# A selective scan's half groups: the copy of two chunks' sums placed two backward steps later, and two delta loads exchanged

## The chip, the cores and the metric

The kernel runs on one core of a Trainium2 chip. The metric is the device time of one execution in microseconds (us), the median of several runs. The engines are TensorE (PE, with its weight loads shown as PEld), VectorE (DVE), ScalarE (ACT), GpSimd (POOL) and SyncE (SP), whose queue issues the DMA transfers.

## The reference

Four layers run over an image batch `x` of shape (4, 64, 64, 96). The change lies in layer 0, which holds a selective scan over 4096 positions in four directions, with 192 channels and 16 states. Cut to what matters:

```python
def step(h, inp):
    u_t, dt_t, B_t, C_t = inp
    dA = jnp.exp(dt_t[..., None] * A)
    h = dA * h + (dt_t * u_t)[..., None] * B_t[:, None, :]
    y = jnp.sum(h * C_t[:, None, :], axis=-1)
    return (h, y)
# ys over all positions, for x_hw, x_wh and both reversed; the four results are added
```

Layer 1 is a depthwise and a pointwise convolution, layer 2 linear attention and a feed-forward block with float quantization, layer 3 a filter between two Fourier transforms and a second feed-forward block. The kernel works on parts of them beside the scan.

## The kernel before

**Tiling.** A tile of the scan has 128 partitions (8 channels by 16 states) and 1024 positions, a *chunk*; four chunks make the 4096 positions. The three indices (image b, orientation o, group g of 8 channels) give N = 4 x 2 x 24 = 192 values of `n`, which this document calls half groups. In each, VectorE scans the four chunks forward (steps q0 to q3, L1700) and then backward (steps k0 to k3, chunks 3 to 0, L1749), and adds the backward result to the forward one (L1759). A backward scan's last value goes to the next through `edge` (L1755).

**What a half group needs.** `load_delta` and `load_du` (both through L1413) fetch a chunk each, in two DMAs of 256 KB. `decay` (L1458, ScalarE) makes exp(delta times A) in PSUM; there are two such buffers, used in turn, and six decays a half group, since those of chunks 2 and 3 serve both directions. `times_b` (L1441) and `times_c` (L1445), on GpSimd, multiply by B and C in place. `reduce` (L1472, PE) adds up the 16 states by matmuls into `py`, one bank of PSUM of which there is a single buffer; `result` (L1480, ScalarE) copies it out, and `store_result` (L1489) stores it with four DMAs. A half group has two such rounds: half 0 for chunks 0 and 1, half 1 for chunks 2 and 3.

**Where the sums stand.** The sums of half 1 of `n` are reduced at k3 of the same half group and copied at q0 of the next. Those of half 0 are reduced in the next half group: chunk 1 at q1, chunk 0 at q3; they are copied at k0, ahead of that step's scan, and stored at k1.

**A second form from half group 55 on.** Once the lane of the other images' preparation is done (`"pre" in done`), the backward scan of chunk 0 writes into the delta tile `dls[n, 0]` instead of being added; `times_c_apart` (L1450) multiplies it, and the reduction of chunk 0 reads it as a second term. The place of that delta tile is then in use until that reduction.

**Places.** Delta tiles have five places, dl0 to dl4. `place_of` gives chunk q the place q in even half groups and 4, 3, 2, 1 in odd ones; the tiles `S` of the scans follow the same rule. So chunks 1 to 3 of the next half group take places of the current one as these come free, and chunk 0 takes the fifth. The du tiles have eight places.

**Order.** The loop writes the order of all engines out by hand (a manual schedule). Every queue runs its instructions in that order, SP's too. After the scan of each step, `pieces(step)` puts in work of the other layers ("pieces" of lanes) as far as the step's credit for each engine goes; its DMAs go through the same SP queue. The loads of the loop on SP, in order, are: q0 du(n+1, 2); q1 du(n+1, 3); q2 delta(n+1, 2) and the store of half 1; q3 delta(n+1, 1); k0 delta(n+1, 0); k1 the store of half 0 and du(n+2, 0); k2 delta(n+1, 3); k3 du(n+2, 1). The decays stand at q0, q1, q2 (chunks 1, 2, 3), k1 (chunk 1 again), k2 (chunk 0 again) and k3 (chunk 0 of n+1).

Of the kernel before, what the change touches and what calls it, by code (L numbers as in the profile page):

```python
# [10 lines left out]
F32 = mybir.dt.float32  # L11
# [35 lines left out]
CH = 1024  # L47
# [26 lines left out]
def layers(ctx: ExitStack, tc: tile.TileContext, a: dict, out):  # L74
# [1294 lines left out]
    def last_place(name, k):  # L1369

        if (name, k) not in last_tiles:
            tags = {
                "w_in": [f"B{4 * (N % 2) + q}" for q in range(4)],
                "sz_in": [f"dl{place_of(*x)}" for x in ((N - 1, 3), (N - 1, 2), (N - 1, 1), (N, 0))],
                "xr": [f"rep0{q}" for q in range(4)],
                "y_in": [f"B{4 - 4 * (N % 2) + q}" for q in range(4)],
            }
            t = big.tile([128, CH], F32, tag=tags[name][k // 2], name=name)
            for j in range(2):
                last_tiles[name, k // 2 * 2 + j] = t[:C, j * BLK : (j + 1) * BLK]  # L1380
        return last_tiles[name, k]
# [16 lines left out]
    N = len(phases)  # L1398
    dls, Bs, Ss, reps, pys, yss = {}, {}, {}, {}, {}, {}

    def place_of(n, q):


        return (4, 3, 2, 1)[q] if n % 2 else q

    def channel_halves(t):

        return [t[k * 64 : k * 64 + 64, :] for k in range(2)]

    def load_channels(t, src, g, q):  # L1410
        for k, part in enumerate(channel_halves(t)):
            rows = src[g * 8 + k * 4 : g * 8 + k * 4 + 4, chunk(q)]
            nc.sync.dma_start(part, rows.unsqueeze(0).broadcast_to([NS, 4, CH]))  # L1413

    def load_delta(n, q):
        if n < N:
            b, g, o = phases[n]
            t = dls[n, q] = big.tile([128, CH], F32, tag=f"dl{place_of(n, q)}", name="dl")
            load_channels(t, delta_s[o][b], g, q)

    def load_du(n, q):
        if n < N:
            b, g, o = phases[n]

            at = 4 * (n % 2) + (3 - q if n % 4 > 1 else q)
            t = Bs[n, q] = big.tile([128, CH], F32, tag=f"B{at}", name="B")
            load_channels(t, du_s[o][b], g, q)
# [24 lines left out]
    def decay(n, q, first):  # L1452

        if n < N:
            tag = "pa" + "XY"[(n + (not first)) % 2]
            pa = ps.tile([128, CH], F32, tag=tag, name="pa")
            g = phases[n][1]
            nc.scalar.activation(pa, dls[n, q], AF.Exp, scale=nega[:, g : g + 1])  # L1458
            return pa

    def reduce(n, half, chunks=(0, 1)):

        if n < 0:
            return
        if (n, half) not in pys:
            pys[n, half] = ps.tile([128, BLK], F32, tag="py", name="py")
        py = pys[n, half]
        for j in (2 * c + k for c in chunks for k in range(2)):
            q, k = 2 * half + j // 2, j % 2
            terms = [Ss[n, q]] + ([dls[n, 0]] if q == 0 and n in apart else [])  # L1470
            for i, x in enumerate(terms):
                nc.tensor.matmul(  # L1472
                    py[32 * j : 32 * j + 32, :], lhsT=red, rhs=x[:, k * BLK : (k + 1) * BLK],
                    start=(i == 0), stop=(i == len(terms) - 1),
                )

    def result(n, half):
        if n >= 0:
            ys = yss[n, half] = big.tile([128, BLK], F32, tag="ys", name="ys", bufs=2)
            nc.scalar.copy(ys, pys.pop((n, half)))  # L1480

    def store_result(n, half):
        if n < 0:
            return
        b, g, o = phases[n]
        ys = yss.pop((n, half))
        for j in range(4):
            i = 4 * half + j
            nc.sync.dma_start(  # L1489
                y_s[o][b][g * 8 : g * 8 + 8, i * BLK : (i + 1) * BLK], ys[32 * j : 32 * j + 8, :]  # L1490
            )
# [114 lines left out]
    big = core.enter_context(tc.tile_pool(name="scan", bufs=1))  # L1606
# [60 lines left out]
    with tc.manual_schedule():  # L1667
        ordered[0] = True
        pas = [decay(0, 0, True), None, None, None]
        for n in range(N + 1):  # L1670
            h = n // NG
            end = n == N

            for q in range(NCH):

                if q < 2:
                    load_du(n + 1, q + 2)
                else:
                    load_delta(n + 1, 4 - q)
                if n % NG == 0 and 0 < n < N and q > 0:  # L1680
                    load_rep(h, 1, 4 - q)
                if q < 3:
                    pas[q + 1] = decay(n, q + 1, q == 1)
                if q == 0:
                    times_b(n, 3)
                elif q == 1:
                    times_c(n - 1, 0)
                    reduce(n - 1, 0, (1,))
                elif q == 2:
                    times_c_apart(n - 1)  # L1690
                    store_result(n - 1, 1)
                else:
                    times_b(n + 1, 0)
                    reduce(n - 1, 0, (0,))
                if end:
                    if q == 0:
                        result(n - 1, 1)
                    continue
                s = Ss[n, q] = big.tile([128, CH], F32, tag=f"S{place_of(n, q)}", name="S")
                nc.vector.tensor_tensor_scan(  # L1700
                    s, pas[q], Bs[n, q], Ss[n, q - 1][:, CH - 1 : CH] if q else 0.0,
                    ALU.mult, ALU.add,
                )
                pieces(q)
                if q == 0:
                    result(n - 1, 1)
            if end:
                result(n - 1, 0)
                store_result(n - 1, 0)
                break  # L1710
            if n % NG == 0 and n > 0:
                load_rep(h, 1, 0)
            if n % NG == 1 and n > 1:
                b, o = halves[h - 1]
                if o == 1:
                    done["columns", b] = True
                if h % 2 == 0 and b < NB - 1:
                    done["scans", b] = True
            if n == N - NG // 2 + 1:
                done["half", NB - 1] = True  # L1720

            for k, q in enumerate(reversed(range(NCH))):
                if k < 2:
                    times_b(n + 1, k + 1)
                if k > 0:
                    times_c(n, q + 1)
                if k == 0:
                    result(n - 1, 0)
                    load_delta(n + 1, 0)
                elif k == 1:  # L1730
                    store_result(n - 1, 0)
                    load_du(n + 2, 0)
                elif k == 2:
                    load_delta(n + 1, 3)
                else:
                    load_du(n + 2, 1)
                if n % NG == NG - 2:
                    load_rep(h + 1, 0, k)
                if k == 1:
                    pas[1] = decay(n, 1, False)  # L1740
                elif k == 2:
                    pas[0] = decay(n, 0, True)
                elif k == 3:
                    first = decay(n + 1, 0, True)


                alone = k == 3 and "pre" in done
                to = dls[n, 0] if alone else pas[q]
                nc.vector.tensor_tensor_scan(  # L1749
                    to[:, ::-1], pas[q][:, ::-1], Bs[n, q][:, ::-1],  # L1750
                    edge if k else 0.0, ALU.mult, ALU.add,
                )
                if k < 3:
                    edge = big.tile([128, 1], F32, tag="edge", name="edge", bufs=2)
                    nc.vector.tensor_copy(edge, to[:, 0:1])  # L1755
                if alone:
                    apart.add(n)
                else:
                    nc.vector.tensor_tensor(Ss[n, q], Ss[n, q], to, ALU.add)  # L1759
                if k == 3:  # L1760
                    reduce(n, 1)
                pieces(4 + k)
                if n == N - 1:
                    for i in (2 * k, 2 * k + 1):
                        last_loads(last_place, i)
            pas[0] = first
            if n % NG == NG - 4 and h + 1 < len(halves):
                b, o = halves[h + 1]
                assert done.get(("turns", b)) if o else done.get(("back", b)) == NBLK, (n, done)
# [118 lines left out]
```

## Time and profile before

| what | value |
|---|---|
| median of 3 runs | 5872.94 us (5869.17 to 5878.88) |
| the profiled execution | 5867.99 us, its span 5866.2 us |
| scan loop within the span | about 359 to 5421 us |
| forward scan, 128x1024 | 2.28 us (first chunk) and 2.35 us |
| backward scan, 128x1024 | 2.30 us (first) and 2.35 us |
| add of both directions | 1.21 us |
| decay on ScalarE | 1.12 us |
| product on GpSimd | 2.36 us |
| copy of half a half group's sums | 0.58 us |
| share of the 16 DMA engines over the span | 72.5% |
| mean granted TensorE clock | 0.778 |

Times are read from one profiled execution. Idle time of an engine is put down to what ended it; a wait for several things is put down to the one that came last. Lines such as L1480 are those of the kernel.

### The profile page before, as it was taken

How to read it: one execution, taken by the hardware profiler on the slowest of the kernel's cores; microseconds unless marked ns; L12 is line 12 of the kernel's file. 1: busy time of each engine (PE TensorE's matmuls, PEld its weight loads, DVE VectorE, ACT ScalarE, POOL GpSimd, SP SyncE). 2: the span in 40 equal slices, each digit the busy share in tenths (PEclk: the TensorE clock that was granted, in tenths of full speed). 3: DMA queues.
4: the chain of work that ended last, by engine and by line, in shares of the span. 5: the costliest groups of instructions: out<-in, count | busy, mean ns of one | idle time of the engine just before them, and what ended most of it. 6: DMA issues, size and time to landing. Idle time of an engine off the chain costs nothing. (4 is left out here: it accounts for less than half of the span.)

```text
span 5866.2 us, 64908 instructions
## 1 busy us (share of the span) xinstructions
PE 4369.5 (74%) x20038; PEld 1680.1 (29%) x20038; DVE 4801.4 (82%) x3479; ACT 3018.7 (51%) x4141; POOL 4413.7 (75%) x2118
## 2 busy tenths in 40 slices
PE   8978898799884776664566776667678667667888
PEld 3322222222220221142331221245222114333345
DVE  2049889889889888999889999999988999979364
ACT  4557666676555346645444546434444554424233
POOL 0258888789879778988778989888897898867200
PEclk9979889899886776666777876668678766767888
DMA  3258868887679878788988867679987578886003
GB/s 100 77 155 237 233 200 229 224 233 214 199 218 246 226 201 224 208 247 239 251 234 227 227 178 214 191 211 251 233 230 205 164 210 233 242 230 194 23 37 105
DMA packets 469417, 1173.13 MB, mean 200 GB/s; under 512 B 90496, under 2 KB 155628, under 8 KB 468972
## 3 DMA queue, kind: packets, MB, share of 16 engines
q1 hardware_dynamic: 469068, 1168.97, 72.5%
q8 instruction: 159, 2.61, 0.2%
q14 instruction: 190, 1.56, 0.1%
HBM read 1011.86 MB, written 156.76 MB: 199 GB/s over the span
## 5 line engine op out<-in xcount | busy, mean ns | idle before, releaser
L1445 POOL TENSOR_TENSOR S<-S,rep 128x1024 f32<-128x1024 f32 x768 | 1807.9, 2356 | 580.6 <-DVE S L1759 496.6
L1441 POOL TENSOR_TENSOR B<-B,rep 128x1024 f32<-128x1024 f32 x768 | 1798.3, 2357 | 107.8 <-DMA B<-du_s 67.8
L1458 ACT ACTIVATE pa<-dl,nega 128x1024 f32<-128x1024 f32 x1152 | 1283.9, 1116 | 1148.3 <-DVE S L1759 717.7
L1700 DVE TENSOR_TENSOR_SCAN S<-pa,S,B 128x1024 f32<-128x1024 f32 x576 | 1352.2, 2348 | 286.8 <-ACT pa L1458 117.2
L1472 PE MATMUL py<-S,red 128*32 128x512 f32 x3072 | 927.4, 845 | 667.2 <-POOL S L1445 456.8
L1749 DVE TENSOR_TENSOR_SCAN pa<-pa,edge,B 128x1024 f32<-128x1024 f32 x439 | 1032.1, 2351 | 67.9 <-ACT pa L1458 67.3
L361 PE MATMUL p_conv<-xp,conv_w 96*96 96x504 f32 (+3 forms) x2304 | 1054.4, 611 | 6.9 <-ACT u L374 4.9
L1759 DVE TENSOR_TENSOR S<-S,pa 128x1024 f32<-128x1024 f32 x631 | 764.7, 1212 | 1.9
L1700 DVE TENSOR_TENSOR_SCAN S<-pa,B 128x1024 f32<-128x1024 f32 x192 | 436.7, 2275 | 225.8 <-ACT pa L1458 179.9
L361 PEld LDWEIGHTS p_conv<-xp,conv_w 96*96 96x96 f32 x2304 | 382.2, 170 | 674.2 <-issue 636.5
L1480 ACT COPY ys<-py 128x512 f32<-128x512 f32 x384 | 222.8, 580 | 546.4 <-PE py L1472 487.3
L1749 DVE TENSOR_TENSOR_SCAN pa<-pa,B 128x1024 f32<-128x1024 f32 x192 | 440.9, 2296 | 5.4
L1472 PEld LDWEIGHTS py<-S,red 128*32 128x32 f32 x3072 | 111.8, 125 | 1148.0 <-POOL S L1445 647.4
L154 ACT COPY side<-side 96x256 f32<-96x256 f32 (+1 forms) x448 | 279.5, 628 | 127.8 <-DMA deltaT_s<-side 46.5
L1749 DVE TENSOR_TENSOR_SCAN dl<-pa,edge,B 128x1024 f32<-128x1024 f32 x137 | 320.7, 2341 | 14.6 <-ACT pa L1458 14.6
L1450 POOL TENSOR_TENSOR dl<-dl,rep 128x1024 f32<-128x1024 f32 x137 | 323.2, 2359 | 0.1
L1055 POOL CAST h<-y 128x1536 fp8e5<-128x1536 f16 x64 | 95.6, 1494 | 296.9 <-ACT y L766 273.6
L1472 PE MATMUL py<-dl,red 128*32 128x512 f32 x548 | 243.5, 752 | 30.3 <-POOL dl L1450 30.1
L877 PE MATMUL p_mean<-t,centre 96*96 96x512 f32 x256 | 172.6, 787 | 98.1 <-ACT sq L869 48.9
L527 PE MATMUL p_y<-side,ident 96*96 96x512 f32 x336 | 208.8, 771 | 24.3 <-DVE q L920 10.0
L833 PE MATMUL p_l<-x,taps 96*96 96x504 f32 (+3 forms) x432 | 202.3, 619 | 14.9 <-DMA x<-x 12.5
L458 POOL TENSOR_TENSOR r<-r,side 96x512 f32<-96x512 f32 x16 | 20.2, 1263 | 249.0 <-ACT side L443 248.8
(214 smaller groups left out, 5580.4 us busy)
## 6 DMA issues: line engine op xcount, KB each, us to landing
B<-du_s SPq DMA_DIRECT2D x768, 256.0 KB
dl<-delta_s SPq DMA_DIRECT2D x768, 256.0 KB
B<-duT_s SPq DMA_DIRECT2D x768, 256.0 KB
dl<-deltaT_s SPq DMA_DIRECT2D x768, 256.0 KB
z_s<-z SPq DMA_DIRECT2D x48, 512.0 KB
zl<-z_s SPq DMA_DIRECT2D x64, 384.0 KB
side<-y_s SPq DMA_DIRECT2D x120, 192.0 KB
rep<-bc_s SPq DMA_DIRECT2D x64, 256.0 KB
```

The costliest lines, as they stand in the source:

```text
L154: nc.scalar.copy(o.rearrange("p (w h) -> p w h", h=HW), t[:n, :].rearrange("p (h w) -> p w h", w=HW)[:, q * w : (q + 1) * w, :],)
L361: nc.tensor.matmul(pr[:, ra:rb, ca_:cb_], lhsT=conv_w[:, kc, ky * 3 + kx, oc * C : (oc + 1) * C], rhs=xp[:, kc, at + ra : at + rb, ca_ + d ...
L527: nc.tensor.matmul(p, lhsT=ident[:C, :C], rhs=x, start=(j == 0), stop=(j == 2))
L1441: nc.gpsimd.tensor_tensor(Bs[n, q], Bs[n, q], reps[n // NG, 0, q], ALU.mult)
L1445: nc.gpsimd.tensor_tensor(Ss[n, q], Ss[n, q], reps[n // NG, 1, q], ALU.mult)
L1450: nc.gpsimd.tensor_tensor(dls[n, 0], dls[n, 0], reps[n // NG, 1, 0], ALU.mult)
L1458: nc.scalar.activation(pa, dls[n, q], AF.Exp, scale=nega[:, g : g + 1])
L1472: nc.tensor.matmul(py[32 * j : 32 * j + 32, :], lhsT=red, rhs=x[:, k * BLK : (k + 1) * BLK], start=(i == 0), stop=(i == len(terms) - 1),)
L1480: nc.scalar.copy(ys, pys.pop((n, half)))
L1700: nc.vector.tensor_tensor_scan(s, pas[q], Bs[n, q], Ss[n, q - 1][:, CH - 1 : CH] if q else 0.0, ALU.mult, ALU.add,)
L1749: nc.vector.tensor_tensor_scan(to[:, ::-1], pas[q][:, ::-1], Bs[n, q][:, ::-1], edge if k else 0.0, ALU.mult, ALU.add,)
L1759: nc.vector.tensor_tensor(Ss[n, q], Ss[n, q], to, ALU.add)
```

## The change

The sums of chunk 0 are reduced at k0 instead of q3; the sums of half 0 are copied at k2 behind that step's decay instead of at k0, and stored at k3 instead of k1. Behind the last half group the same three steps stand one after another. Delta of chunk 0 of the next half group is loaded at q2 instead of k0, and delta of chunk 2 at k1 instead of q2; chunks 1 and 3 keep their steps. The delta places follow a list in place of `place_of`: the next half group's chunks 0 to 3 take the places of the current chunks 2 and 3, the spare place and the place of chunk 1, and the current chunk 0's becomes spare. The tiles `S` keep `place_of`. The place of one group of late loads for the end of the kernel (`sz_in`) is named by the same list.

```diff
-                "sz_in": [f"dl{place_of(*x)}" for x in ((N - 1, 3), (N - 1, 2), (N - 1, 1), (N, 0))],
+                "sz_in": [
+                    f"dl{delta_places[n][q]}" for n, q in ((N - 1, 3), (N - 1, 2), (N - 1, 1), (N, 2))
+                ],
...
+    delta_places, spare = [(0, 1, 2, 3)], 4
+    while len(delta_places) <= N:
+        p = delta_places[-1]
+        delta_places.append((p[2], p[3], spare, p[1]))
+        spare = p[0]
...
-            t = dls[n, q] = big.tile([128, CH], F32, tag=f"dl{place_of(n, q)}", name="dl")
+            t = dls[n, q] = big.tile([128, CH], F32, tag=f"dl{delta_places[n][q]}", name="dl")
...
                 if q < 2:
                     load_du(n + 1, q + 2)
                 else:
-                    load_delta(n + 1, 4 - q)
+                    load_delta(n + 1, q - 2)
...
                 else:
                     times_b(n + 1, 0)
-                    reduce(n - 1, 0, (0,))
...
             if end:
+                reduce(n - 1, 0, (0,))
                 result(n - 1, 0)
                 store_result(n - 1, 0)
...
                 if k == 0:
-                    result(n - 1, 0)
-                    load_delta(n + 1, 0)
+                    reduce(n - 1, 0, (0,))
                 elif k == 1:
-                    store_result(n - 1, 0)
                     load_du(n + 2, 0)
+                    load_delta(n + 1, 2)
                 elif k == 2:
                     load_delta(n + 1, 3)
                 else:
+                    store_result(n - 1, 0)
                     load_du(n + 2, 1)
...
                 elif k == 2:
                     pas[0] = decay(n, 0, True)
+                    result(n - 1, 0)
```

## The prediction

> **What bounds the kernel now.** I read the page first (busy times and the costliest groups), then the stretches before and after the reductions get their second matmul pair, then who waits for the copy and for the queue, and last the timeline around single stalls.
>
> ```profile
> PE 4369.5 (74%) x20038; PEld 1680.1 (29%) x20038; DVE 4801.4 (82%) x3479; ACT 3018.7 (51%) x4141; POOL 4413.7 (75%) x2118
> ...
> L1700 DVE TENSOR_TENSOR_SCAN S<-pa,S,B 128x1024 f32<-128x1024 f32 x576 | 1352.2, 2348 | 286.8 <-ACT pa L1458 117.2
> ...
> L1749 DVE TENSOR_TENSOR_SCAN pa<-pa,edge,B 128x1024 f32<-128x1024 f32 x439 | 1032.1, 2351 | 67.9 <-ACT pa L1458 67.3
> ...
> L1480 ACT COPY ys<-py 128x512 f32<-128x512 f32 x384 | 222.8, 580 | 546.4 <-PE py L1472 487.3
> ```
>
> VectorE carries the scans, and nothing overlaps a scan of the same engine. The windows of the two stretches of the scan loop show its load there:
>
> ```profile
> 359.00:1861.00 1502.00, 1249.38 (x3098) 385.35 (x3099) 1314.61 (x840) 963.51 (x1312) 1284.57 (x646) 0.85 0.79 221
> 1861.00:5421.00 3560.00, 2435.56 (x12872) 970.85 (x12870) 3239.71 (x2230) 1717.29 (x2322) 2984.45 (x1361) 0.72 0.81 220
> ```
>
> The columns are length, then PE, PEld, DVE, ACT, POOL busy, clock, DMA share, GB/s. VectorE is busy 1314.6 of 1502 us (87.5%) and 3239.7 of 3560 us (91%), so about 187 + 320 = 507 us of its idle time lie in the loop. Only idle time of VectorE can be won. Two kinds of it touch the change. The first, from the timeline of half group 12:
>
> ```profile
> 688.49 1.05 PE L1472 MATMUL py<-S,red 128*32 128x512 f32 x4
> ...
> 689.59 0.58 ACT L1480 COPY ys<-py 128x512 f32<-128x512 f32 x1 [7.89 <-PE py L1472]
> 690.19 1.28 ACT L399 ACT_TABLE_LOAD   x1
> ...
> 693.51 1.28 ACT L107 ACT_TABLE_LOAD   x1
> 694.80 1.12 ACT L1458 ACTIVATE pa<-dl,nega 128x1024 f32<-128x1024 f32 x1
> ...
> 695.96 2.36 DVE L1749 TENSOR_TENSOR_SCAN pa<-pa,edge,B 128x1024 f32<-128x1024 f32 x1 [2.87 <-ACT pa L1458]
> ```
>
> The copy of step k0 stands at ScalarE's head for 7.89 us until PE reaches the reduction of chunk 0; four other instructions and the decay of k1 are queued behind it, and the backward scan of k2 starts 2.87 us late. The second, from half group 60:
>
> ```profile
> 1958.56 1.16 SPq L1413 DMA_DIRECT2D dl<-deltaT_s  x2
> ...
> 1965.57 2.15 ACT L1458 ACTIVATE pa<-dl,nega 128x1024 f32<-128x1024 f32 x2 [9.89 <-DMA dl<-deltaT_s]
> ...
> 1966.78 2.29 DVE L1700 TENSOR_TENSOR_SCAN S<-pa,B 128x1024 f32<-128x1024 f32 x1 [6.40 <-issue]
> ```
>
> Here delta of chunk 0 is issued late, lands at about 1965.5, and the next half group's first scan loses 6.40 us. The DMA queue's own waits name two that the change moves (total us, times, longest):
>
> ```profile
> SPq L1413 <- PE py L1472: 182.5, 61, 10.2
> ...
> SPq L1489 <- ACT ys L1480: 117.3, 44, 9.2
> ```
>
> **What the Trainium skill says.** "PSUM — Partial Sum Buffer", Engine vs sequencer instructions: the queues of ScalarE, VectorE and GpSimd are strict FIFO. The 7.89 us above agrees: work that needs nothing from PE waits behind the copy. "DMA: Bandwidth & Descriptors", Anatomy of one DMA: a semaphore wait happens on the issuing sequencer, before dispatch. The 182.5 us agree: one load that waits for PE holds every load behind it. "ScalarE: Activation LUTs", What ACT_TABLE_LOAD costs: about 1283 ns a load, and a drain besides; the trace has 1.28 us, twice in the chain above. "Perfetto Trace Analysis", Optimization Strategy: find the gaps on the contended engine and the instruction that ends them, which is how the sums below are made.
>
> **The change part by part.** No instruction is added or removed; steps are q0 to q3 (forward) and k0 to k3 (backward).
>
> 1. *Copy of chunks 0 and 1 from k0 to k2, behind the last decay.* Taking all scans of the loop in order, and calling a scan stalled when its idle time exceeds 0.32 us and its decay ended within 0.25 us of its start: in the first 55 half groups the scan of k2 is stalled 25 times, 52.9 us in all (the later ones: 7 times, 9.4 us). Following each back along ScalarE's order, the copy's wait stands in the chain in 21 of the 25, with 40.4 us. With the copy at k2 the table load, two activations and a table load (1.28+1.06+1.04+1.28 us) can start up to 8 us earlier, as in half group 12, so the stall itself goes. What is late next in that stretch is PE: forward scans there already wait 14.3 us for reductions, and PE is busy 83%. I take three quarters of 40.4: **30 us** (10 to 45).
>
> 2. *The copy in its new place.* It is 0.58 us of ScalarE behind the decay of chunk 0 and ahead of the pieces of k2. That decay can start when the scan of k2 starts (k1's add is over), 7.1 us after k0's first scan. PE ends the reduction of chunk 0 at a median of 1.3 us after that scan in the first stretch (90%: 4.3, worst 7.7), 0.2 in the second (90%: 3.7). Moved behind pieces(3), whose PE credit is 2.0, I add 2 to 4 us: at worst 11.7, mostly under 8. So the copy seldom waits, and the next half group's first decay, which needs k2's add at 10.7, hides it. The reduction of chunks 2 and 3 at k3 needs the same single bank of PSUM, free at about 7.1+1.1+0.6 = 8.8 us, but also the product of chunk 2 on GpSimd, ready at 7.1+2.36 = 9.5: nothing. Without that cover it would cost PE 1 to 2 us a half group, which VectorE would see only in part.
>
> 3. *Reduction of chunk 0 from q3 to k0.* Its matmuls had 38 us of PE waiting ahead of them in all (4.6 and 33.8 us by stretch); pieces(3) no longer stand behind that. Nothing else: 0 us (-5 to +5).
>
> 4. *Delta of chunk 0 from k0 to q2.* It goes to the place of the current chunk 2, free after the decay of q1, some 7 us ahead of k0, so it has 18 us to land where it had 11 less the wait for PE. Late arrivals of it now: 16 stalls of the next first scan, 42.5 us, all in the second stretch. They go.
>
> 5. *Delta of chunk 2 from q2 to k1.* It takes the spare place, which the reduction of chunk 0 frees in the half groups with the separate product, and it is queued behind du of n+2. Queued behind its wait for PE: delta 3, the store, du and the pieces' transfers. The du load it now follows was issued 5.8 us (median), 9.0 (75%) and 12.7 (90%) after k0's scan in the second stretch; ahead of it a delta load and a store (1.2 and 1.3 us) disappear. A delta load takes 5.3 us to land (median), and the decay has to start by 16.9 us, so it must be issued by about 11. That leaves nearly a tenth of 136 half groups, 13, late by 2 us: 26 us back on f2. Also, the stretches with late loads have the DMA engines at 86 to 93% and delta 3 lands there with 0 to 3 us to spare, so part of item 4 only moves on to q2's scans. Net of 4 and 5: 42.5 - 26 = 16, less a little for delta 3: **13 us** (-60 to +45; the lower end is the rival below).
>
> 6. *Store from k1 to k3.* Four issues, 1.3 us; the wait of 117.3 us for the copy leaves du of k1. The du load of k3 now stands behind it, at 8.8 us or later, where it was issued at a median of 10 to 11: within 2 us, hidden by GpSimd's waits for VectorE (496.6 us over the run). 0 us (-10 to 0).
>
> Sum: 30 + 13 = 43 us. The profiled execution took 5867.99 us (span 5866.2, 1.8 around it): 5825. The median shown, 5872.94, is 5 us above that execution, so **5830 us**.
>
> **The rivals.**
> - *A, as above, in whole or in part*, 15 to 75 us won: 5830, own range 5798 to 5858. For it: the stalls are on VectorE itself and their causes are in the moved instructions.
> - *B, all of it and more.* The 42.5 and 40.4 us go whole, and with them 14.3 us of stalls by delta 3 at q3, since the queue isn't held at k0: 97 us, 5776. Against it: a late queue in those stretches has other causes (ScalarE's decays alone hold it 268.0 us).
> - *C, refilled.* What is won at k2 is lost at the next forward scans to PE, and what is won at the first scan to the DMA engines: within 10 us of 5873. For it: PE at 83% in the first stretch, DMA at 90% where loads are late.
> - *D, slower: delta of chunk 2 becomes the late load.* Place: the decay of q1 and the scan of q2. It decides when the load at k1 is issued later than 11 us after k0's scan in over a quarter of the second stretch: 35 half groups by 3 us are 105 us, less the 72 of items 1 and 4: 33 us slower, 5906. For it: one more load is queued ahead of it than of chunk 0 before, its place hangs on PE, and delta 3, issued right behind it, is already late 13 times. Against it: the decay of q1 comes 5 us later than the one it replaces as the tightest.
>
> **How the numbers follow.** A 0.55, B 0.10, C 0.14, D 0.21. A change of 0.2%, 12 us, is about what can be told from none. A and B win more than that nearly always: faster 0.66. C is mostly inside it: same 0.13. Slower 0.21. The range for 8 in 10 takes A, C, half of B and most of D: 5785 to 5898.
>
> **What would show it.** Item 1: idle time of L1749 for decays falls from 67.3 us to under 25, and the copies' wait for PE from 487.3 to under 150. Item 4: no first forward scan waits for delta. Item 5: decays of q1 that wait for delta, none today; over 30 of them, or over 60 us, prove D. If the waits fall but the idle time of L1700 grows by as much, C is right.

## The result and the profile after

The changed kernel took 5849.50 us (5844.06 to 5857.01, 5 runs), against 5872.96 us before (5 runs): ratio 0.9965, 95% interval 0.9952 to 0.9978. It is 23 us faster, where the forecast was 43. Two later measurements of the same kernel, each beside the kernel before on the same chip, gave 0.9943 (0.992 to 0.9965, 28 us) and 0.9949 (0.9929 to 0.9968, 33 us). So by the medians the gain is 23 to 33 us, and 10 to 20 us of the forecast are missing. (The ratios are not the quotients of these medians; by them the three gains are 21, 33 and 30 us, and their intervals together reach from 13 to 47 us.)

These lines of the page of the changed kernel answer to those shown of before (L1708 is now the forward scan, L1759 the backward scan, L1467 the decay, L1481 the reduction, L1489 the copy, L1422 the loads, L1498 the store, L1769 the add):

```profile
PE 4352.3 (74%) x20038; PEld 1673.5 (29%) x20038; DVE 4799.4 (82%) x3479; ACT 3016.6 (52%) x4141; POOL 4412.4 (75%) x2118
...
L1708 DVE TENSOR_TENSOR_SCAN S<-pa,S,B 128x1024 f32<-128x1024 f32 x576 | 1352.2, 2348 | 316.2 <-ACT pa L1467 146.0
...
L1759 DVE TENSOR_TENSOR_SCAN pa<-pa,edge,B 128x1024 f32<-128x1024 f32 x439 | 1031.9, 2351 | 40.4 <-ACT pa L1467 40.4
...
L1489 ACT COPY ys<-py 128x512 f32<-128x512 f32 x384 | 221.8, 578 | 9.8 <-PE py L1481 7.5
```

The copies no longer wait for PE: 487.3 us became 7.5. Of the 67.3 us that the backward scans lost to decays, 27 are gone. But the forward scans of q1 to q3 now lose 146.0 us to decays instead of 117.2: more than what the backward scans won. The gain lies elsewhere, in the first forward scans, whose line is this before and then after:

```profile
L1700 DVE TENSOR_TENSOR_SCAN S<-pa,B 128x1024 f32<-128x1024 f32 x192 | 436.7, 2275 | 225.8 <-ACT pa L1458 179.9
```

```profile
L1708 DVE TENSOR_TENSOR_SCAN S<-pa,B 128x1024 f32<-128x1024 f32 x192 | 436.4, 2273 | 188.9 <-DMA rep<-bc_s 169.8
```

Their idle time fell by 36.9 us. (One wait of about 170 us at the start of the loop is in both.) The windows of the two stretches say where the time changed; the first stretch ends at the first scan of half group 56, and the columns are as before:

```profile
358.30:1857.80 1499.50, 1253.00 (x3092) 387.92 (x3096) 1313.68 (x840) 964.04 (x1312) 1282.25 (x646) 0.85 0.80 221
1857.80:5402.60 3544.80, 2411.72 (x12879) 961.67 (x12873) 3238.12 (x2230) 1714.31 (x2322) 2985.02 (x1361) 0.73 0.82 221
```

The first stretch, where the copy's 30 us were to be won, is only 2 us shorter; the second, where only delta was to win, is 15 us shorter. (By the means of all profiles in the table below, three of the changed kernel and two of before, it is 10 and 19 us.) The single cases shown of before are both cured. Half group 12, in the timeline:

```profile
687.94 2.30 DVE L1759 TENSOR_TENSOR_SCAN pa<-pa,B 128x1024 f32<-128x1024 f32 x1
...
691.10 1.05 PE L1481 MATMUL py<-S,red 128*32 128x512 f32 x4
691.48 2.35 DVE L1759 TENSOR_TENSOR_SCAN pa<-pa,edge,B 128x1024 f32<-128x1024 f32 x1
...
695.07 2.35 DVE L1759 TENSOR_TENSOR_SCAN pa<-pa,edge,B 128x1024 f32<-128x1024 f32 x1
695.19 1.12 ACT L1467 ACTIVATE pa<-dl,nega 128x1024 f32<-128x1024 f32 x1 [2.12 <-DVE S L1769]
696.24 0.58 ACT L1489 COPY ys<-py 128x512 f32<-128x512 f32 x1
```

The reduction ends at 692.15, 4.2 us after the scan of k0 begins; nobody waits for it, and the copy follows the decay of k2 without a gap. The scan of k2 (695.07) stands directly behind k1's add. And half group 60, whose first scan lost 6.40 us to delta:

```profile
1948.86 1.53 SPq L1422 DMA_DIRECT2D dl<-deltaT_s  x2
...
1955.52 1.12 ACT L1467 ACTIVATE pa<-dl,nega 128x1024 f32<-128x1024 f32 x1 [1.96 <-DVE S L1769]
1957.66 2.27 DVE L1708 TENSOR_TENSOR_SCAN S<-pa,B 128x1024 f32<-128x1024 f32 x1
```

The decay now waits for VectorE's own add, and the first scan starts without idle time.

For what follows, each scan ahead of which VectorE stood idle for over 0.32 us is counted by its step and by the cause, as in the prediction; the wait of 170 us at the start of the loop is left out. "Late" means that the scan's decay ended within 0.25 us of the scan's start; "delta" means that this decay had itself waited for a load of delta. "PE idle" is time in which PE did nothing ahead of an instruction of one set, summed over 54 half groups of the first stretch: the reduction of chunk 0 and the pieces of q3, which are the work that the change puts in the other order. All values are us of one profiled execution each.

| kernel | first stretch | k2 late | q0 + q1 late | PE idle | second stretch | q0 delta | q2, q3 delta |
|---|---|---|---|---|---|---|---|
| before | 1501.9 | 52.9 | 12.0 | 6.9 | 3559.9 | 42.5 | 14.4 |
| before, second profile | 1505.4 | 56.5 | 10.9 | 8.1 | 3560.0 | 43.7 | 11.4 |
| changed | 1499.5 | 24.7 | 36.7 | 17.9 | 3544.8 | 0 | 43.6 |
| changed, second | 1493.2 | 24.2 | 28.7 | 17.8 | 3539.8 | 0 | 41.0 |
| changed, third | 1489.5 | 20.7 | 26.1 | 19.0 | 3539.0 | 0 | 38.9 |
| sums_only | 1495.7 | 30.0 | 24.8 | 20.7 | 3559.7 | 54.1 | 11.2 |
| copy_only | 1479.6 | 23.1 | 14.7 | 8.3 | 3574.5 | 54.7 | 13.4 |
| deltas_only | 1512.1 | 52.8 | 17.2 | 7.2 | 3547.5 | 0 | 45.7 |
| sum_at_q3 | 1483.4 | 26.5 | 17.5 | 5.2 | 3548.7 | 0 | 44.4 |
| sum_at_q3, second | 1478.3 | 23.8 | 17.4 | 8.2 | 3549.8 | 0 | 39.5 |
| sum_at_q3_d2_k0 | 1477.6 | 26.3 | 12.4 | 7.9 | 3541.4 | 0 | 25.1 |
| first_q3 | 1492.4 | 29.4 | 19.4 | 6.5 | 3529.8 | 0 | 32.4 |
| sum_at_k1 | 1493.2 | 25.4 | 36.2 | - | 3539.6 | 0 | 39.6 |
| reduction_alone | 1535.4 | 108.6 | 6.2 | 16.5 | 3573.0 | 33.0 | 14.3 |

A row stands for one execution, which need not be a typical one: that of copy_only took 5867.38 us, the longest of its 19 (median 5848.43), that of sum_at_q3 5842.53, the longest of its 6 (5832.15), and that of sum_at_k1 5841.17, the shortest of its 22 (5855.66).

Two things stand in the rows of the changed kernel. The stall of k2 fell by 28 to 32 us, as forecast, and late decays of q0 and q1, which grew by 14 to 25 us, took much of it back.

### The profile page after: what moved, and what is told of

Its sections match the earlier page's. It is cut to its first block, busy times and chain, and to the rows that moved or that the text cites. A ratio compares the mean times of both kernels' runs of the same rounds, so it can differ in the third digit from the quotient of the medians.

```text
span 5852.6 us, 65288 instructions
## 1 busy us (share of the span) xinstructions
PE 4352.3 (74%) x20038; PEld 1673.5 (29%) x20038; DVE 4799.4 (82%) x3479; ACT 3016.6 (52%) x4141; POOL 4412.4 (75%) x2118
## 5 line engine op out<-in xcount | busy, mean ns | idle before, releaser
L1467 ACT ACTIVATE pa<-dl,nega 128x1024 f32<-128x1024 f32 x1152 | 1286.0, 1117 | 1448.0 <-DVE S L1769 1089.6
L1708 DVE TENSOR_TENSOR_SCAN S<-pa,S,B 128x1024 f32<-128x1024 f32 x576 | 1352.2, 2348 | 316.2 <-ACT pa L1467 146.0
L1481 PE MATMUL py<-S,red 128*32 128x512 f32 x3072 | 894.9, 837 | 673.6 <-POOL S L1454 460.9
L1759 DVE TENSOR_TENSOR_SCAN pa<-pa,edge,B 128x1024 f32<-128x1024 f32 x439 | 1031.9, 2351 | 40.4 <-ACT pa L1467 40.4
L1769 DVE TENSOR_TENSOR S<-S,pa 128x1024 f32<-128x1024 f32 x631 | 764.6, 1212 | 1.9
L1708 DVE TENSOR_TENSOR_SCAN S<-pa,B 128x1024 f32<-128x1024 f32 x192 | 436.4, 2273 | 188.9 <-DMA rep<-bc_s 169.8
L1759 DVE TENSOR_TENSOR_SCAN pa<-pa,B 128x1024 f32<-128x1024 f32 x192 | 440.8, 2296 | 5.4
L1481 PEld LDWEIGHTS py<-S,red 128*32 128x32 f32 x3072 | 108.5, 124 | 1142.0 <-POOL S L1454 629.7
L1759 DVE TENSOR_TENSOR_SCAN dl<-pa,edge,B 128x1024 f32<-128x1024 f32 x137 | 320.7, 2341 | 18.3 <-ACT pa L1467 11.2
L527 PE MATMUL p_y<-side,ident 96*96 96x512 f32 x336 | 217.6, 798 | 41.5 <-DVE side L561 12.4
L1481 PE MATMUL py<-dl,red 128*32 128x512 f32 x548 | 222.7, 736 | 21.2 <-POOL dl L1459 21.2
L1489 ACT COPY ys<-py 128x512 f32<-128x512 f32 x384 | 221.8, 578 | 9.8 <-PE py L1481 7.5
```

Source lines behind the costliest of these rows:

```text
L1481: nc.tensor.matmul(py[32 * j : 32 * j + 32, :], lhsT=red, rhs=x[:, k * BLK : (k + 1) * BLK], start=(i == 0), stop=(i == len(terms) - 1),)
L1708: nc.vector.tensor_tensor_scan(s, pas[q], Bs[n, q], Ss[n, q - 1][:, CH - 1 : CH] if q else 0.0, ALU.mult, ALU.add,)
L1759: nc.vector.tensor_tensor_scan(to[:, ::-1], pas[q][:, ::-1], Bs[n, q][:, ::-1], edge if k else 0.0, ALU.mult, ALU.add,)
```

## The experiments

Three theories were on record. P: PE paces the first stretch whatever the order, so what is won at k2 is lost at the next forward scans (rival C of the prediction). R: it is the reduction, moved from q3 to k0, that makes PE late for those scans. S: the small gain of the first stretch is scatter of one execution. Every experiment below was timed beside the kernel before on the same chip.

**The change taken apart.** The changed kernel again, and its parts alone:

```diff
# sums_only: reduction k0, copy k2, store k3 of the change; delta loads and places as before
# copy_only: as sums_only, and the reduction stays at q3
                     times_b(n + 1, 0)
+                    reduce(n - 1, 0, (0,))
...
                 if k == 0:
-                    reduce(n - 1, 0, (0,))
                     load_delta(n + 1, 0)
# deltas_only: delta loads and places of the change; reduction q3, copy k0, store k1 as before
```

> The changed kernel once more, for the spread of one profiled execution. The first stretch of the scan loop (to the first scan of half group 56) lasted 1501.9 us before and 1499.5 us after, the second 3559.9 and 3544.8 us. Theory P (in the first stretch PE, with the stretches in which its clock is lowered, sets the pace, so that the stall taken from the scan of k2 comes back at the next forward scans): first stretch again 1496 to 1502 us. Rival S (the first stretch is won in most executions and was not in the one profiled): 1475 to 1490 us. Both: ratio to before 0.995 to 0.998.

> Reduction of chunk 0, copy and store moved as in the change; delta loads and places as before. P: nothing won in the first stretch (1496 to 1502 us); in the second, the load of delta 0 at k0 now waits for a reduction that comes 1 to 3 us later, so first forward scans lose more to delta than the 42.5 us of before: whole time 0 to 15 us over before. Rival S: 10 to 25 us won in the first stretch, whole time 5855 to 5870.

> Only the copy (k0 to k2) and the store (k1 to k3) moved; the reduction of chunk 0 stays at q3, delta loads as before. P: first stretch 1495 to 1502 us, whole time within 8 us of before. Rival R (the refill comes from the reduction, which in its new place stands in PE's queue ahead of the next group of convolution matmuls): the first stretch keeps the gain, 1472 to 1485 us, whole time 5845 to 5858.

> Only delta loads and places changed; reduction at q3, copy at k0 and store at k1 as before. All theories: first stretch as before (1498 to 1505 us), copies wait for PE about 487 us as before. P: the second stretch alone carries the gain of the change, 12 to 25 us, whole time 5848 to 5861. S and R: it carries less than that, 0 to 12 us.

Measured, against 5868.31 us for the kernel before: after_again 5840.74 (0.9943, 0.992 to 0.9965); sums_only 5865.22 (0.9993, 0.9983 to 1.0003); copy_only 5848.43 (0.9964, 0.9952 to 0.9976); deltas_only 5860.36 (0.9985, 0.9975 to 0.9995).

The copy alone (with the store) wins 20 us. With the reduction moved as well, only 3 us are left; the two intervals don't overlap, and the two kernels differ in that one step. A later reduction could also have held up the load of delta at k0, as the expectation of sums_only had it, but the first scans' waits for delta are the same in both, 54.1 and 54.7 us. P fails for copy_only: its k2 stalls fell to 23.1 us, q0 and q1 stayed at 14.7, and the first stretch was 22 us shorter than before. (In that one long execution the second stretch was 15 us longer than before, so the 20 us rest on the median of 19 executions.) The deltas alone win 8 us, which fits all three theories.

S was right in part. after_again's first stretch, 1493.2 us, lies between what P and S expected, and its ratio is below the expected 0.995. But the first stretch of sums_only, 1495.7 us, is at the edge of P's bounds and far from the 10 to 25 us that S expected to be won there.

**The change without the moved reduction.**

```diff
# sum_at_q3, against the changed kernel
                     times_b(n + 1, 0)
+                    reduce(n - 1, 0, (0,))
...
             if end:
-                reduce(n - 1, 0, (0,))
                 result(n - 1, 0)
...
                 if k == 0:
-                    reduce(n - 1, 0, (0,))
+                    pass
# sum_at_q3_d2_k0: as above, and
                 if k == 0:
+                    load_delta(n + 1, 2)
                 elif k == 1:
                     load_du(n + 2, 0)
-                    load_delta(n + 1, 2)
```

> The whole change but for one step: the reduction of chunk 0 stays at q3; copy at k2, store at k3 and both delta loads as in the change. R (the moved reduction stands in the middle of PE's convolution work and gives back what the copy wins): 10 us or more below the changed kernel, 5820 to 5838 us against 5868 before (ratio 0.992 to 0.995), the first stretch below 1490 us. P (PE with its half-clock episodes paces the first stretch whatever the order): as the changed kernel, 5840 to 5850, first stretch 1493 to 1500. S (what was seen is scatter from run to run): within 5 us of the changed kernel, either side.

> As sum_at_q3, and delta of chunk 2 is loaded at k0, a step sooner than in the change (its place is free there once the reduction stands at q3). If the load is late because it is issued behind du at k1, the second stretch's waits of the scans of q2 and q3 for delta, 43.6 us in the changed kernel, fall below 15 us and the kernel is 20 to 30 us below sum_at_q3. If the DMA engines are what is late (they are at 86 to 93% there), the waits stay above 30 us or come back at the first scan, and the time is within 8 us of sum_at_q3.

Measured, against 5868.98: sum_at_q3 5832.15 (0.9929, 0.9909 to 0.9948), sum_at_q3_d2_k0 5831.45 (0.9931, 0.9912 to 0.9949). As R expected, 37 us below before, and the first stretch at 1483.4 and 1477.6. Loading delta of chunk 2 a step sooner cured the waits of q2 (20.6 us to none) but not those of q3 (23.8 and 25.1), so the waits fell from 44.4 to 25.1 us and not to under 15, and the time did not move. The window of the first stretch of sum_at_q3:

```profile
357.00:1840.40 1483.40, 1238.41 (x3092) 383.82 (x3096) 1313.51 (x840) 963.63 (x1312) 1282.50 (x646) 0.85 0.80 224
```

What the reduction does at q3 and at k0 is to be seen in half group 41. First the timeline of the changed kernel, then that of sum_at_q3, at the same step:

```profile
1465.64 2.71 PE L361 MATMUL p_conv<-xp,conv_w 96*96 96x512 f32 x6
...
1468.98 0.91 ACT L305 ACTIVATE xb<-xb,gn 96x640 f32<-96x640 f32 x1
...
1469.94 0.78 PE L313 MATMUL p_xp<-xb,w_in 96*96 96x320 f32 x2 [1.58 <-ACT xb L305]
1470.65 1.20 PE L1481 MATMUL py<-S,red 128*32 128x512 f32 x4
...
1471.78 2.02 PE L361 MATMUL p_conv<-xp,conv_w 96*96 96x512 f32 x2
```

```profile
1453.64 2.71 PE L361 MATMUL p_conv<-xp,conv_w 96*96 96x512 f32 x6
...
1456.28 1.05 PE L1481 MATMUL py<-S,red 128*32 128x512 f32 x4
...
1456.98 0.91 ACT L305 ACTIVATE xb<-xb,gn 96x640 f32<-96x640 f32 x1
...
1457.94 0.78 PE L313 MATMUL p_xp<-xb,w_in 96*96 96x320 f32 x2 [0.60 <-ACT xb L305]
1458.56 2.73 PE L361 MATMUL p_conv<-xp,conv_w 96*96 96x512 f32 x6
```

PE runs its work in the written order. In the first stretch this order is the same in both kernels, but for the place of the moved reduction. At q3 PE has to wait for ScalarE's `xb` in any case. With the reduction at q3 its 1.05 us lie in that wait, and 0.60 us of idle time are left. With the reduction at k0 PE idles for 1.58 us and does the reduction afterwards, ahead of the next convolution. The same 0.60 against 1.58 us stands in half groups 20, 22, 37, 39 and 41 of both kernels; two others (17, 49) have 1.41 against none, where PE waits for ScalarE's `r`. The table's column "PE idle" sums it up: 5.2 to 8.3 us in all kernels with the reduction at q3, 16.5 to 20.7 with it at k0. (The last line of the changed kernel's timeline is slow for another reason: the granted clock was 0.50 there, and 1.00 in the last line of sum_at_q3's.)

PE's lateness shows at the half groups right behind, in four of five cases. By the mean, 21, 38, 40 and 42 take 1.4 to 2.7 us longer in the kernels with the copy at k2 and the reduction at k0 (the changed kernel three times, sums_only) than in those with it at q3 (copy_only, sum_at_q3 twice, sum_at_q3_d2_k0, first_q3). In these four half groups late decays of q0 and q1 cost 7.0 to 13.7 us with the reduction at k0, and 0 to 1.5 us with it at q3. Over the whole first stretch they cost 29.1 us by the mean against 16.3. Following ScalarE's order back from each of these late decays, its last wait was one for PE in 21 to 29 us of them with the reduction at k0, and in 10 to 12 us with it at q3. So the 13 us between the two sets come by way of PE. The granted clock doesn't tell them apart: it is 0.85 to 0.86 over the first stretch in all nine profiles.

**What PE's time is worth.** In both kernels 8 of the 18 matmuls of each convolution of images 1 to 3 are left out, so that their sums are no longer those of the reference:

```diff
                         at = r0 + dy - lo
+                        if b > 0 and k % 2 and k < 17:
+                            continue
                         nc.tensor.matmul(
```

> Before, with 8 of the 18 matmuls of each convolution of images 1 to 3 left out (the credit they are counted at is kept, so the order stays): PE has some 375 us less to do in the first stretch. P: PE paces a good part of the stretch, so it becomes at least 60 us shorter (5868 to 5810 or less). R: PE only delays what stands behind it at single places: 15 to 50 us shorter. The wait of the copies for PE at k0 must fall under both, since PE reaches the reduction sooner: to under 250 us.

> The changed kernel with the same 8 of 18 matmuls left out. P and R: with PE's load gone the moved reduction costs nothing, and the copy's stall at k2 is smaller in both kernels; what is left of the difference to before_light is the delta part, 9 us, plus what of the copy's wait was not PE's load: 5 to 20 us below before_light. If instead the reduction at k0 costs time for a reason other than PE's queue, after_light is not below before_light.

Measured: before_light 5777.49 (0.9839, 0.9824 to 0.9855), after_light 5764.81 (0.9825, 0.9807 to 0.9843). The first stretches, before_light and after_light:

```profile
359.20:1775.10 1415.90, 1028.43 (x2330) 278.38 (x2331) 1312.29 (x839) 965.81 (x1312) 1283.05 (x646) 0.75 0.84 235
```

```profile
356.80:1773.60 1416.80, 1020.58 (x2329) 276.88 (x2329) 1312.04 (x840) 963.96 (x1312) 1282.81 (x646) 0.75 0.83 234
```

With 221 us less PE work (1249 to 1028; the expected 375 was too much) the stretch is 86 us shorter, where R expected 15 to 50 and P at least 60, and the two kernels are equal in it. With PE at 73% the copy at k0 costs no more than that at k2 (stalls of k2: 14.0 us in before_light, 18.0 in after_light), although copies still wait 52.6 us for PE in that stretch (136.3 before), and the moved reduction costs nothing either (late decays of q0 and q1: 7.8 and 8.1 us). The 12.7 us between the two lie in the second stretch (3557.0 and 3538.5). The copies' total wait only fell to 416.3 us, against the expected 250, since most of it is in the second stretch, which the edit doesn't touch. So P is right in one point: both the gain and the loss of the first stretch need PE's load. Each microsecond of its work left out there shortened the stretch by 0.39 us.

**Pairs on one chip, and other places.**

```diff
# first_q3, against the changed kernel
                     times_b(n + 1, 0)
+                    if n - 1 not in apart:
+                        reduce(n - 1, 0, (0,))
...
                 if k == 0:
-                    reduce(n - 1, 0, (0,))
+                    if n - 1 in apart:
+                        reduce(n - 1, 0, (0,))
# sum_at_k1, against the changed kernel
                 if k == 0:
-                    reduce(n - 1, 0, (0,))
+                    pass
                 elif k == 1:
+                    reduce(n - 1, 0, (0,))
                     load_du(n + 2, 0)
```

> The changed kernel unaltered, beside the runs below on one chip: 5840 to 5850 us against about 5868 before (ratio 0.995 to 0.9965), first stretch 1493 to 1500 us.

> The change without the move of the reduction of chunk 0, beside the changed kernel on one chip. R (the moved reduction gives part of the win back): again 0.991 to 0.995 of before, 8 to 20 us below the changed kernel here. If the first result was chance, within 5 us of it.

> The change, with the reduction of chunk 0 at q3 in the first stretch (while its second term doesn't exist) and at k0 in the second. If what the move costs lies in the first stretch alone, where PE is loaded, the time is that of the kernel with the reduction at q3 throughout: 0.991 to 0.995, first stretch 1475 to 1487 us, second 3538 to 3550. If it lies in the second, it is that of the changed kernel, 0.995 to 0.9965.

> The changed kernel with the reduction of chunk 0 one step later still, at k1. If the cost comes from where the four matmuls stand among the other work of PE, it is here as large as at k0 or larger: the first stretch at 1493 us or more, with the stalls of the scan of q1 at 20 us or more, and the copies at k2 wait for PE 15 to 60 us in all; the time 0.995 to 1.0 of before. If k0 alone is a bad place, the first stretch falls below 1490 us.

Measured, against 5870.98: after_third 5837.60 (0.9949, 0.9929 to 0.9968), sum_at_q3_again 5836.01 (0.9947, 0.9928 to 0.9965), first_q3 5828.89 (0.9931, 0.9912 to 0.9949), sum_at_k1 5855.66 (0.9979, 0.9969 to 0.9989).

after_third came out 2 us below its expected time, and its first stretch 3 us below the expected one. The direct pair missed: sum_at_q3_again is within 2 us of the changed kernel. Its first stretch is 11 us shorter (1478.3 against 1489.5), as R says, but its second is 11 us longer. One stall there, 2.5 us of q1 at half group 127, is in both profiles of this kernel and in none of the changed kernel; the rest of the 11 us has no cause that the runs show.

That second stretch is shorter with the reduction at k0 in every pair of profiles with the copy at k2: 3559.7 us (sums_only) against 3574.5 (copy_only) with the old delta loads, 3539.0 to 3544.8 (changed) and 3529.8 (first_q3) against 3548.7 and 3549.8 (sum_at_q3) with the new. So the move may win in the second stretch what it loses in the first, which would make the direct pair even. No run tries that apart; the medians of sums_only and copy_only speak against it, and so does reduction_alone below (3573.0 against 3559.9 before).

first_q3 was to join the two good halves. Its time, the lowest of all kernels with the full computation, fits that, but its first stretch came out at 1492.4, outside the expected 1475 to 1487, although sum_at_q3 has the same order there and took 1483.4 and 1478.3. So a single profile of the stretch scatters by some 6 us. That first_q3 beats the changed kernel is not shown; the intervals of the two overlap. One step later still, at k1, the reduction costs more, as expected of its place: 18 us above the changed kernel by the medians. Late decays at q0 and q1 cost 36.2 us, 27.4 of them at q1 (at least 20 were expected), and the copies wait 38.0 us for PE (15 to 60).

**The move alone.**

```diff
                     times_b(n + 1, 0)
-                    reduce(n - 1, 0, (0,))
...
             if end:
+                reduce(n - 1, 0, (0,))
                 result(n - 1, 0)
...
                 if k == 0:
+                    reduce(n - 1, 0, (0,))
                     result(n - 1, 0)
```

> Before, with the reduction of chunk 0 moved from q3 to k0 and nothing else; the copy still follows at k0. R: the scans of q0 and q1 of the first stretch lose 8 to 18 us more to late decays than before (12.0 us there), as in all kernels with the reduction at k0 or k1; and since the copy at k0 now waits for a reduction that ends some 2 us later, the scan of k2 stalls for 55 to 90 us instead of 52.9. Together 15 to 50 us slower: 5885 to 5920. If the move costs nothing by itself (item 3 of the prediction), the stalls of q0 and q1 stay at 9 to 18 us, and only those of k2 grow.

> The kernel before, unaltered, for a second profile of it: total 5862 to 5880, first stretch 1498 to 1512 us, stalls of the scan of k2 50 to 56 us and of those of q0 and q1 by late decays 9 to 18 us. If the first stretch comes out at 1495 or below, the difference of 12 us between kernels with the reduction at q3 and at k0 is not to be told from scatter.

Measured, against 5865.62: reduction_alone 5926.48 (1.0112, 1.0097 to 1.0126), before_again 5869.13 (1.0002, 0.9993 to 1.0011). The page of reduction_alone:

```profile
L1699 DVE TENSOR_TENSOR_SCAN S<-pa,S,B 128x1024 f32<-128x1024 f32 x576 | 1352.6, 2348 | 266.4 <-ACT pa L1458 109.3
...
L1750 DVE TENSOR_TENSOR_SCAN pa<-pa,edge,B 128x1024 f32<-128x1024 f32 x439 | 1032.3, 2351 | 132.0 <-ACT pa L1458 132.0
...
L1480 ACT COPY ys<-py 128x512 f32<-128x512 f32 x384 | 223.3, 581 | 727.1 <-PE py L1472 651.2
```

With the copy at k0 the move costs 61 us, more than expected, and at another place than expected: it stands at k2, where the copies' wait grew to 651.2 us and the backward scans' loss to 132.0; q0 and q1 lose only 6.2 us, less than before, and nothing in half groups 21, 38, 40 and 42. So the expectation for q0 and q1 failed, which corrects R. A reading that fits is that PE catches up while VectorE stands still at k2 for 108.6 us in the first stretch, and is no longer late half a period further on: PE's lateness is paid at the first instruction that meets it, and with the copy at k2 this is no longer k2 but q0 and q1. PE idled 16.5 us in the same set, as in the other kernels with the reduction at k0. before_again confirms the baseline: 1505.4 us, k2 56.5, q0 and q1 10.9.

## Why the prediction was wrong in size

- **Item 1, the copy (30 us): right in its mechanism, too large as time.** The stall of k2 fell from 52.9 to 24.7, 24.2 and 20.7 us, 28 to 32 us. But the five profiles with the copy moved and the reduction at q3 have a first stretch of 1482.3 us by the mean, 21 us below before (1503.7): late decays of q0 to q2 grow by 8 us with the copy alone. copy_only was 20 us faster by the median. The marker "under 25" for L1749 was set too low for the prediction's own sum: three quarters of 40.4 leave 23 us in the first stretch and those of the second besides; 40.4 were measured.
- **Item 2, the copy's new place (0): right.** The copies wait 7.5 us for PE.
- **Item 3, the reduction (0, -5 to +5): wrong, and the step that failed.** The prediction said of the move: "pieces(3) no longer stand behind that. Nothing else". It counted what stands behind the reduction and not what the reduction fills. (Its 38 us of PE waiting ahead of these matmuls were also too few: PE's idle time directly ahead of them is 3 us in the first stretch and 63 in the second.) At q3 its 1.05 us lay in PE's waits for ScalarE; at k0 they don't, and PE idles 11 us more in the first stretch (6.9 to 17.9). Late decays at q0 and q1 grew from 12.0 to 36.7, 28.7 and 26.1 us, where kernels with the copy moved and the reduction left at q3 have 12.4 to 19.4. In place of 0 the move thus costs some 13 us there, and the first stretch is 12 us longer by the means (1494.5 against 1482.3). In the whole time this was 17 us between sums_only and copy_only, and could not be told from nothing in the pair of changed kernel and sum_at_q3_again. In the second stretch PE idles more by the same exchange of order, too (67 and 70 us before, 85 to 89 in the changed kernel), but that stretch did not become longer; PE is busy for 68% of it. So the mechanism and its size in the first stretch are shown by the profiles; what it is worth in the total is uncertain, some 2 to 17 us, and whether the second stretch gives part of it back is open.
- **Items 4 and 5, the deltas (net 13 us): right, part by part.** No first scan of the second stretch waits for delta (42.5 us gone). Delta of chunk 2 is late 12 times for 22.5 us, where 13 times and 26 us were forecast, and delta 3 at q3 costs 6.7 us more (14.4 to 21.1): net 13.3. ScalarE waited for delta ahead of the decay at q1 20 times, 51.0 us, under the bounds of 30 times and 60 us, and the kernel is faster, so rival D is refuted. The second stretch as a whole is 19 us shorter by the means, 5 us more than these stalls. In the total, deltas_only gained 8 us; its second stretch is 12 us shorter, its first 7 to 10 us above the two profiles of before.
- **Item 6, the store (0): not tried by itself.** SP's wait of the store for the copy grew:

```profile
SPq L1498 <- ACT ys L1489: 184.6, 98, 9.0
```

From 117.3 us, that is. In copy_only and sums_only, which have the store at k3 and the old delta loads, first scans of the second stretch lost 54.7 and 54.1 us to delta, against 42.5 and 43.7 before. So the place of the store, or of the copy that it waits for, seems not to be free there; in the changed kernel, whose delta of chunk 0 is loaded at q2, no first scan waits for delta.

- **Rival C** was right that the next forward scans take something back, some 8 us with the reduction at q3 and 22 with it at k0, but not that all of it is lost: copy_only and sum_at_q3 keep most of it. The sign that the prediction named for C did appear: the idle time of L1700 grew by 29.4 us (286.8 to 316.2) while that of L1749 fell by 27.5. Of that growth 16 us stand in the first stretch; in the second, delta of chunks 2 and 3 alone adds 29 us and other waits fall. The sign mixes what C and item 5 foretold, and so can't prove C.
- **The sum.** The first stretch won 21 us by the copy and lost 12 by the reduction, the second won 19: 28 us, against 23 to 33 measured.

## What to carry to other kernels

An instruction in an in-order queue is cheap where the queue would wait anyway: before moving one, look at what its engine does at the old place (does it fill a wait?) and not only at who waits for it. What a microsecond of such an engine is worth depends on where it stands: here 11 us more of PE's idle time went with a first stretch 12 us longer, 221 us less of PE's work shortened it by only 86, and some 19 us more of idle time in the second stretch cost nothing that shows. When a late engine is no longer met at one place, look for the next place where its results are needed, and count the lateness there.

## What was not expected of the hardware

With 221 us less work for PE in the first stretch, its mean granted clock there was lower, 0.75 instead of 0.85 (both light kernels), so a lighter load did not buy a faster clock. The clock records hold 1.0 and 0.5, in turns, and the same convolution matmul takes two lengths: in the two timelines of half group 41 above, 2 records take 2.02 us in the changed kernel, at a granted clock of 0.50, and 6 take 2.73 us in sum_at_q3, at 1.00. Executions of the changed kernel scatter with a standard deviation of 10 us (17 executions, 5822.48 to 5859.15), and single profiles of its first stretch from 1489.5 to 1499.5.
